# Row norms from statistics, factors in two parts of 16 and 6 tiles, and a mean row summed on VectorE in a two-layer graph kernel

## The chip, the core and the metric

The kernel runs on one core of a Trainium2 chip. A core has five engines with a queue of instructions each: TensorE (PE, with the weight load PEld beside it), VectorE (DVE), ScalarE (ACT), GpSimd (POOL) and SyncE (SP), which issues transfers. Every engine takes its instructions in order, and an instruction waits until what it reads has been written and the buffer that it writes is free. The metric is the time of one execution on the device in microseconds, lower is better.

## The reference

Two layers work on 2,708 rows of 256 numbers and a 2,708 x 2,708 graph. Each is an attention over the graph and then a mixture of experts with two experts for every row. The change lies in layer 1's attention, which works in hyperbolic space:

```
c = float(k)                                   # 1
logx = logmap0(x, c)                           # acosh(x[:,0]) * y / |y|, y = x[:,1:]
Wx = logx[:, 1:] @ W_gcn
tmp = concatenate([0, Wx])
fun7 = proj(expmap0(tmp, c), c)
h_in = logmap0(fun7, c)
h = h_in @ W_att
e = h @ a_att[:F_] + (h @ a_att[F_:]).T
att = softmax(where(adj > 0, e, MASK_FILL), axis=1)
emb = proj(elu(att @ h), c)
out = expmap0(sigmoid(logmap0(emb, c)), c)
```

with x the layer-normed rows. All the maps only scale a row, so `h` of a row is the row through one joined matrix, times a factor that is worked out from three numbers: the row's first element, the norm of its other elements, and the norm of its projection without the second matrix. The softmax's weight then splits: a term that depends on the row read is folded into that row's factor `p_scale`, and the rest drops out. A row with no neighbour gets the mean of all `h`; it comes in through an additional row of the last column with a tiny weight.

## The kernel before

**Tiles.** The rows lie in 22 tiles of 128 (the last two have 74), `tiles`; two neighbours are a pair, 11 in all. `LAST` is 21. The mask of the graph stands in SBUF as `mask_t`, one byte each. Column j of a row tile i is the part of the mask between the tiles j and i.

**Queues.** Instructions of TensorE, VectorE, ScalarE and SyncE keep the order in which the program issues them (L152); those of GpSimd are put in order by the scheduler. Work up to the attention is issued by `Turns`: pieces are generators, each `step()` advances every due piece to its next `yield`, older pieces first. From the attention's third tile on, work is issued by `Clock`: each piece names an engine and an estimated time before it issues, and the planner takes the piece that could start first; `Slots` and `Mark` stand for buffers and events in it. Its estimates set only the order.

**Preparing layer 1.** While layer 0's last experts run, `ahead` (L1461) normalizes the first four pairs and takes the squares of their rows on ScalarE (`square_rows`, L1456) into `norms[:, 0]`. After layer 0 a table of functions is loaded into ScalarE (L1513). `prepare1` adds the two sums of a pair on GpSimd, takes its statistics, and normalizes it on VectorE; `project1` (L1563) turns the pair on TensorE, copies it to `xts` on ScalarE, squares its rows there, projects it (8 matmuls into `u_ps`, of which there are three), squares the projection into `norms[:, 1]` and evicts it to `h_all`. The loop at L1666 starts a pair at each step. In steps 6 to 9 it widens the mask of the row tiles 0 and 1 from bytes to words (`widen`, L1521): the odd columns on GpSimd, the even ones on ScalarE. There are four such half masks.

**Factors.** `factors1(lo, n)` (L1592) turns the three numbers of n tiles into `scale` and `p_scale`: some 35 small VectorE instructions in a chain, with a logarithm and exponents on ScalarE in between. Before, it runs for tiles 0 to 11 within the loop (`FIRST` is 12), started after step 11, and for 12 to 21 after it. `split` (L1634) writes `h * p_scale` of a tile as a rounded half (ScalarE) and its remainder (VectorE), which are the two operands `halves` of the attention.

**Attention.** `sum_up(i, j)` (L1644) adds column j to row tile i with two matmuls of 258 columns. There are three accumulators of the tag `acc` in PSUM. The program issues columns 0 to 11 for the row tiles 0 and 1, then `add_h` (L1653), 44 matmuls that sum `scale * h` of all rows into the mean row, then the second splits, the last column with the mean row in its partitions 64 to 95 (L1691), and the columns 12 to 21. `attention` (L1750) goes on with tile 2 to 21, each with even columns first; `widener` widens the masks, `finish1` (L1763) closes a tile (reciprocal, activation, sum of squares). When the six tiles of a group are closed, `points1` takes them to the router; after the second group (tiles 0 to 11) the first expert blocks of layer 1 are planned, fetched and run.

Of the kernel before, what the change touches and what calls it, by code (L numbers as in the profile page):

```python
# [9 lines left out]
F32 = mybir.dt.float32  # L10
F32R = mybir.dt.float32r
# [11 lines left out]
P = 128  # L23
# [123 lines left out]
def kernel(  # L147
# [260 lines left out]
    def log1p(u):  # L408

        t = ts(u, 1.0, OP.add)  # L410
        k = ts(t.bitcast(I32), 23, OP.logical_shift_right, dtype=I32)
        down = ts(k, -1.0, OP.mult, 254.0, OP.add, dtype=I32)
        scale = ts(down, 23, OP.logical_shift_left, dtype=I32).bitcast(F32)
        m = tt(tt(u, scale, OP.mult), ts(scale, -1.0, OP.add), OP.add)
        z = tt(m, recip(ts(m, 2.0, OP.add)), OP.mult)
        z2 = tt(z, z, OP.mult)
        terms = [2.0 / (2 * n + 1) for n in range(8)]
        q = ts(z2, terms[7], OP.mult)
        for c in reversed(terms[1:7]):
            q = sts(q, c, OP.add, z2, OP.mult)  # L420
        q = sts(q, terms[0], OP.add, z, OP.mult)
        return tt(ts(k, -127.0, OP.add, math.log(2.0), OP.mult), q, OP.add)
# [1033 lines left out]
    def square_rows(xp, pair):  # L1456
        for q, (t, r) in enumerate(pair):
            nc.scalar.activation(row_tile("junk", 4)[:r, 1:], xp[q][:r, 1:], AF.Square,
                                 accum_out=norms[:r, 0, t:t + 1])

    def ahead(b):  # L1461
# [21 lines left out]
        if left == 0:  # L1483
            for k, pair in enumerate(pairs[:AHEAD - 1]):
                square_rows(normed[k], pair)
# [24 lines left out]
    halves = [att.tile([P, T, D + 2], F32R, name=f"half{k}") for k in range(2)]  # L1510
    zeros = filled("zeros", 0.0, T, pool=att)
# [51 lines left out]
    def project1(pair, xp):  # L1563
        ps = ps_tile("tr_ps", "tr").rearrange("p (t c n) -> p t c n", c=DC, n=P)
        for q, (t, r) in enumerate(pair):
            turn_rows(xp[q][:r], r, ps[:, q])
            nc.gpsimd.tensor_copy(c0[:r, t:t + 1], xp[q][:r, 0:1])
        yield 1
        xt = row.tile([P, 2, DC, P], F32, name="xts", bufs=2)
        if pair[1][1] == P:  # L1570
            nc.scalar.copy(xt, ps)
        else:
            for q, (t, r) in enumerate(pair):
                nc.scalar.copy(xt[:, q, :, :r], ps[:, q, :, :r])
        if pairs.index(pair) >= AHEAD - 1:
            square_rows(xp, pair)
        yield 1
        us = []
        for q, (t, r) in enumerate(pair):
            us.append(ps_tile("u_ps", "u"))  # L1580
            project(us[q][:r], xt[:, q], w1x, r)
        yield 1
        for q, (t, r) in enumerate(pair):
            nc.scalar.activation(row_tile("junk", 4)[:r, 1:], us[q][:r, :D - 1], AF.Square,
                                 accum_out=norms[:r, 1, t:t + 1])
            nc.scalar.copy(h_all[:r, t, :], us[q][:r, D - 1:])  # L1586
# [5 lines left out]
    def factors1(lo, n):  # L1592
# [3 lines left out]

# [8 lines left out]
        yield 1  # L1605
        y = newton(v, y)
        u = tt(tt(v[:, :n], y[:, :n], OP.mult), d, OP.add)
        f = tt(log1p(u), y[:, n:2 * n], OP.mult)
        wx = tt(tt(v[:, 2 * n:], y[:, 2 * n:], OP.mult), f, OP.mult)
        part = sts(wx, LEAST, OP.max, recip(ts(wx, MIN_NORM, OP.max)), OP.mult)  # L1610
        tt(part, f, OP.mult, scale[:, lo:hi])
        score = tt(scale[:, lo:hi], h_all[:, lo:hi, D], OP.mult)
        nc.scalar.activation(p_all[:, lo:hi], score, AF.Exp)
        yield 1
# [29 lines left out]
    def sum_up(i, j):  # L1644
# [3 lines left out]
        for half_k in halves:  # L1648
            nc.tensor.matmul(accs[i][:, :D + 2], wide_masks[i, j % 2][:k, j // 2, :],  # L1649
# [3 lines left out]
    def add_h(mean, lo, hi):  # L1653

        for t, r in tiles[lo:hi]:
            nc.tensor.matmul(mean[:96, :D], scale[:r, t:t + 1].to_broadcast([r, 96]),
                             h_all[:r, t, :D], start=t == 0, stop=t == LAST)

    turns = Turns()
    FIRST = 12  # L1660
# [6 lines left out]
    for k in range(17):  # L1667
# [3 lines left out]
        if 6 <= k < 10:  # L1671
            widen(k % 2, k < 8)

        if k == FIRST // 2 - AHEAD + 10:
            turns.start(factors1(0, FIRST))
        if k >= 14:
            lo = 4 * (k - 14)
            split_h(lo, lo + 4)
    split_h(lo + 4, FIRST)
    turns.start(factors1(FIRST, T - FIRST))  # L1680
    turns.finish()
    psum_stage(wide=5, acc=3)
    mean = ps_tile("mean_ps")
# [3 lines left out]
    add_h(mean, 0, T)  # L1687
    split_h(FIRST, FIRST + 4)
    split_h(FIRST + 4, LAST)
    nc.scalar.preload_act_table_set(TANH_TABLE)  # L1690
    split(LAST, slice(64, 96), mean[64:96, :D], TINY / N)  # L1691
    split(LAST, slice(0, TAIL), h_all[:TAIL, LAST, :D], p_scale[:TAIL, LAST:])
    for part in range(2):
        for t in range(FIRST + part, T, 2):
# [55 lines left out]
    def attention():  # L1750
        for i in range(2, T):
            acc_slots[i] = yield from acc.get()
            accs[i] = ps_tile("att_ps", "acc")
            for part in range(2):
                yield wide_at[i, part]
                for j in range(part, T, 2):
# [3 lines left out]
            clock.start(finish1(*tiles[i]), 0)  # L1760
        att_scope.close()
        late_pools()
        clock.set(started)  # L1763

# [255 lines left out]
    for t in range(2):  # L2020
        clock.start(finish1(*tiles[t]), 0)
# [56 lines left out]
```

## Time and profile before

| what | value |
|---|---|
| median of three runs | 1162.97 us (1161.6 to 1166.65) |
| the profiled execution | 1136.56 us, its span 1134.8 us |
| mean granted clock of TensorE | 0.958 |
| layer 0's last expert matmul starts | 657.50 us after the span's start |
| projections of layer 1 | 662.2 to 708.8 us |
| attention of layer 1 on TensorE | 710.4 to 862.5 us |
| first expert block of layer 1 on TensorE | 880.05 us |
| last expert output read by VectorE | about 1094 us |

In the lines of the timeline the columns are the start and the duration in microseconds, the engine, the source line, the operation, what is written and read with its size, how many instructions are merged, and in brackets the idle time of the engine before them and what ended it. The granted clock of a stretch is a share of full speed. The profiled execution is 26.4 us, 2.3%, below the median of the timed runs, so differences are taken within the trace and then laid on the median.

### The profile page before, as it was taken

What the parts mean: (1) busy time and instruction counts of PE and PEld (TensorE: products, weight loads), DVE (VectorE), ACT (ScalarE), POOL (GpSimd) and SP (SyncE); (2) the same over time, 40 slices, a digit from 0 to 9 for tenths busy, and PEclk for the clock granted to TensorE, in tenths of its full rate; (3) what the DMA queues carried; (4) which work ended last, traced back from release to release, by engine and by line L of the source; (5) the groups of instructions that cost most, each with busy time, mean ns of one, the idle gap of its engine ahead of it and who ended that gap; (6) DMA issues with size and microseconds to landing.
All of it is one profiled execution on the core that took longest, in us unless ns stands there. A gap on an engine that the chain in (4) does not pass through costs nothing. (4 is left out here: it accounts for less than half of the span.)

```text
span 1134.8 us, 21254 instructions
## 1 busy us (share of the span) xinstructions
PE 1023.5 (90%) x6665; PEld 909.0 (80%) x6665; DVE 541.9 (48%) x2083; ACT 572.7 (50%) x1599; POOL 367.1 (32%) x417
## 2 busy tenths in 40 slices
PE   5999999998999999999999999998984888999950
PEld 3788888886889999999998853898984787898840
DVE  7778888887420111111111235647777552122368
ACT  4867667664524444444443357536754543444320
POOL 7531112111242222212222350253345166433442
PEclk9999999999989999999999999999897889999985
DMA  9965354431889999999899959400225477787974
GB/s 289 288 242 177 136 175 156 166 95 58 303 251 295 327 326 322 323 306 321 257 311 335 340 160 278 150 1 6 76 84 153 124 215 188 187 213 178 282 194 133
DMA packets 165461, 238.96 MB, mean 211 GB/s; under 512 B 11035, under 2 KB 140374, under 8 KB 162632
## 3 DMA queue, kind: packets, MB, share of 16 engines
q1 hardware_dynamic: 146524, 214.09, 57.9%
q0 software_dynamic: 18816, 23.42, 10.6%
q8 instruction: 56, 0.92, 0.3%
q14 instruction: 65, 0.53, 0.2%
HBM read 205.54 MB, written 54.99 MB: 230 GB/s over the span
## 5 line engine op out<-in xcount | busy, mean ns | idle before, releaser
L911 DVE TENSOR_SCALAR yo<-out_ps,w 128x256 f32<-128x256 f32 x92 | 44.5, 483 | 402.4 <-PE out_ps L905 401.9
L1246 PE MATMUL att_ps<-g_all,z 128*128 128x257 f32 (+3 forms) x968 | 223.6, 383 | 0.0
L905 PE MATMUL out_ps<-room,ht 128*128 128x256 f32 x872 | 201.1, 383 | 0.0
L1246 PEld LDWEIGHTS att_ps<-g_all,z 128*128 128x128 f32 (+3 forms) x968 | 174.9, 186 | 29.6 <-issue 3.1
L887 PEld LDWEIGHTS hid_ps<-xt,room 128*128 128x128 f32 x1504 | 176.4, 193 | 7.3 <-issue 2.5
L887 PE MATMUL hid_ps<-xt,room 128*128 128x128 f32 x1504 | 177.7, 277 | 4.2 <-DMA room<-in_L_ffn_W_dram 3.7
L905 PEld LDWEIGHTS out_ps<-room,ht 128*128 128x128 f32 x872 | 162.7, 192 | 21.3
L1232 ACT ACTIVATE zr<-e_bc,minus_one,g_all 128x256 f32<-128x256 f32 (+3 forms) x242 | 130.4, 591 | 46.4 <-DVE z L1235 45.8
L916 POOL DMA_INDIRECT sums<-yo,xg x43 | 66.8, 1554 | 235.0 <-DVE side L879 173.4
L891 ACT ACTIVATE ht<-hid_ps,w_t 128x128 f32<-128x128 f32 x376 | 128.7, 364 | 28.0 <-PE hid_ps L887 8.8
L681 POOL DMA_INDIRECT rows_d<-xr,place x88 | 92.2, 1048 | 121.0 <-DVE xr L450 76.9
L1649 PE MATMUL att_ps<-half,wide_mask 128*128 128x258 f32 (+1 forms) x968 | 124.5, 290 | 2.5 <-ACT h_all L1586 1.5
L1649 PEld LDWEIGHTS att_ps<-half,wide_mask 128*128 128x128 f32 (+1 forms) x968 | 121.5, 195 | 3.9 <-ACT h_all L1586 2.4
L1235 DVE SCALAR_TENSOR_TENSOR z<-zr,mask_t 128x256 f32<-128x256 f32 (+3 forms) x242 | 96.9, 422 | 29.6 <-ACT zr L1232 18.3
L916 POOL DMA_INDIRECT sums<-yo,xr x45 | 70.6, 1569 | 118.0 <-DMA sums<-yo,xr 30.0
L891 ACT ACTIVATE ht<-hid_ps,w1x 128x128 f32<-128x128 f32 x180 | 62.4, 363 | 88.6 <-PE hid_ps L887 85.0
L881 ACT ACTIVATE w<-xg,side 128x1 f32<-128x1 f32 x43 | 12.7, 294 | 169.2 <-DVE side L879 169.2
L1525 POOL CAST wide_mask<-mask_t 128x1408 fp32r<-128x1408 fp8e4 x31 | 42.5, 1375 | 101.6 <-PE att_ps L1649 67.5
L887 PE MATMUL hid_ps<-lo,wide_mask 128*128 128x128 f32 x480 | 63.4, 287 | 5.6 <-DMA wide_mask<-in_L_ffn_w_dram 4.7
L887 PEld LDWEIGHTS hid_ps<-lo,wide_mask 128*128 128x128 f32 x480 | 60.6, 200 | 9.4 <-issue 6.5
L905 PE MATMUL out_ps<-wide_mask,ht 128*128 128x256 f32 x240 | 59.6, 393 | 0.0
L468 PE MATMUL tr_ps<-ident,xr 128*128 128x128 f32 (+1 forms) x214 | 38.2, 289 | 22.2 <-DMA xr<-rows_d 13.9
(292 smaller groups left out, 1325.0 us busy)
## 6 DMA issues: line engine op xcount, KB each, us to landing
room<-in_L_ffn_W_dram SPq DMA_DIRECT2D x94, 1024.0 KB
wide_mask<-in_L_ffn_w_dram SPq DMA_DIRECT2D x60, 512.0 KB
room<-in_adj_dram SPq DMA_DIRECT2D x20, 1354.0 KB
room<-in_L_ffn_w_dram SPq DMA_DIRECT2D x30, 512.0 KB
rows_d<-nobody SPq DMA_DIRECT2D x1, 7511.0 KB
rows_d<-nobody SPq DMA_DIRECT2D x5, 1295.0 KB
sums<-nobody SPq DMA_DIRECT2D x2, 2944.0 KB
xr<-rows_d SPq DMA_DIRECT2D x45, 129.5 KB
```

The source lines that it names most:

```text
L468: nc.tensor.transpose(ps[:, c, :r], src[:, c * P:(c + 1) * P], ident[:r, :r])
L681: ins = nc.gpsimd.indirect_dma_start(out=self.rows_d[:, :], in_=self.rows[t][:r], in_offset=None, out_offset=bass.IndirectOffsetOnAxis(ap= ...
L887: nc.tensor.matmul(ps[:, :P], w1_b[:, c, f * P:(f + 1) * P], xt[:, c, :], start=(c == 0), stop=(c == DC - 1))
L891: nc.scalar.activation(ht[:, f, :], ps[:, :P], self.func, bias=self.bias[:, f, b:b + 1])
L905: nc.tensor.matmul(ps[:, :D], ht[:, f, :], self.rooms[b % 3][1][:, f, :], start=False, stop=(f == self.FC - 1))
L911: nc.vector.tensor_scalar(yo, ps[:, :D], w, None, op0=OP.mult)
L916: ins = nc.gpsimd.indirect_dma_start(out=self.sums[k][:, :], in_=yo, in_offset=None, out_offset=bass.IndirectOffsetOnAxis(ap=self.rows.pop ...
L1232: nc.scalar.activation(zr[:k, :n], e_bc[:k, lo:lo + n], AF.Relu, bias=minus_one[:k], scale=g_all[:k, j, D + 1:D + 2])
L1235: nc.vector.scalar_tensor_tensor(z[:k, :n], zr[:k, :n], 1.0, mask_t[:k, j // 2, lo:lo + n, j % 2], op0=OP.add, op1=OP.mult)
L1246: nc.tensor.matmul(accs[i][:r, :D + 1], z[:k, q * P:q * P + r], g_all[:k, j, :D + 1], start=(j == 0), stop=(j == LAST))
L1525: nc.gpsimd.tensor_copy(m, src)
L1649: nc.tensor.matmul(accs[i][:, :D + 2], wide_masks[i, j % 2][:k, j // 2, :], half_k[:k, j, :], start=(j == 0 and half_k is halves[0]), stop ...
```

## The change

- The squares of the rows on ScalarE go. `factors1` computes the norm from the layer norm's variance and deviation: 256 times variance times deviation squared, less the first element's square.
- `factors1` and `log1p` yield after almost every step. `FIRST` is 16: the first factors cover tiles 0 to 15 and are issued from step 13 on, twelve steps in each round; the second cover 16 to 21, ten of their steps are put between the splits of tiles 6 to 15, and the others behind them.
- All four half masks of row tiles 0 and 1 are widened on GpSimd.
- `add_h` sums `scale * h` tile by tile on VectorE into `h_sum`; one matmul with ones then gives the mean row.
- That matmul stands behind row tile 2, so row tiles 0 to 2 (`OPEN`) get their last column while tile 3 is summed. Their masks for it are copied to `last_masks`, tile 3 takes an accumulator of the other tag, and `finish1` of the three starts after it. The planner is told that VectorE is busy for its first 6 us.

```diff
     def log1p(u):
         t = ts(u, 1.0, OP.add)
+        yield
         k = ts(t.bitcast(I32), 23, OP.logical_shift_right, dtype=I32)
+        yield
...
-    def square_rows(xp, pair):
-        for q, (t, r) in enumerate(pair):
-            nc.scalar.activation(row_tile("junk", 4)[:r, 1:], xp[q][:r, 1:], AF.Square,
-                                 accum_out=norms[:r, 0, t:t + 1])
-
...
-        if left == 0:
-            for k, pair in enumerate(pairs[:AHEAD - 1]):
-                square_rows(normed[k], pair)
...
+    OPEN = 3
...
-        if pairs.index(pair) >= AHEAD - 1:
-            square_rows(xp, pair)
...
+        var, dev, first = ln_a1.mv[:, lo:hi, 1], ln_a1.rstd[:, lo:hi], c0[:, lo:hi]
+        rest = tt(sts(var, float(D), OP.mult, dev, OP.mult), dev, OP.mult)
+        tt(rest, tt(first, first, OP.mult), OP.subtract, norms[:, 0, lo:hi])
+        yield
...
         nc.scalar.activation(y, v, AF.Ln)
         nc.scalar.activation(y, y, AF.Exp, scale=-0.5)
-        yield 1
-        y = newton(v, y)
-        u = tt(tt(v[:, :n], y[:, :n], OP.mult), d, OP.add)
+        yield
+        h = sts(v, 0.0, OP.add, y, OP.mult)
+        yield
...
         for half_k in halves:
-            nc.tensor.matmul(accs[i][:, :D + 2], wide_masks[i, j % 2][:k, j // 2, :],
+            late = j == LAST and i < OPEN
+            nc.tensor.matmul(accs[i][:, :D + 2],
+                             last_masks[i][:k] if late else wide_masks[i, j % 2][:k, j // 2, :],
                              half_k[:k, j, :], start=(j == 0 and half_k is halves[0]),
                              stop=(j == LAST and half_k is halves[1]))
 
-    def add_h(mean, lo, hi):
-
-        for t, r in tiles[lo:hi]:
-            nc.tensor.matmul(mean[:96, :D], scale[:r, t:t + 1].to_broadcast([r, 96]),
-                             h_all[:r, t, :D], start=t == 0, stop=t == LAST)
+    def add_h(h_sum, t, r):
+        if t == 0:
+            nc.vector.tensor_scalar(h_sum, h_all[:, t, :D], scale[:, t:t + 1], None, op0=OP.mult)
+        else:
+            nc.vector.scalar_tensor_tensor(h_sum[:r], h_all[:r, t, :D], scale[:r, t:t + 1],
+                                           h_sum[:r], op0=OP.mult, op1=OP.add)
 
     turns = Turns()
-    FIRST = 12
+    FIRST, START1 = 16, 13
...
-    for k in range(17):
+    near = factors1(0, FIRST)
+    for k in range(18):
...
         if 6 <= k < 10:
-            widen(k % 2, k < 8)
-
-        if k == FIRST // 2 - AHEAD + 10:
-            turns.start(factors1(0, FIRST))
-        if k >= 14:
-            lo = 4 * (k - 14)
-            split_h(lo, lo + 4)
-    split_h(lo + 4, FIRST)
-    turns.start(factors1(FIRST, T - FIRST))
+            widen(k % 2, k < 8, pool=True)
+        if k >= START1:
+            for _ in range(12):
+                next(near, None)
+    for _ in near:
+        pass
     turns.finish()
     psum_stage(wide=5, acc=3)
-    mean = ps_tile("mean_ps")
+    far = factors1(FIRST, T - FIRST)
+    for t in range(FIRST):
+        split_h(t, t + 1)
+        if t >= 6:
+            next(far)
+    for _ in far:
+        pass
     for j in range(FIRST):
         for i in range(2):
             sum_up(i, j)
-    add_h(mean, 0, T)
-    split_h(FIRST, FIRST + 4)
-    split_h(FIRST + 4, LAST)
+    split_h(FIRST, LAST)
+    h_sum, last_masks = xr_tile()[:, :D], []
+    for i in range(OPEN):
+        if i % 2 == 0:
+            two = xr_tile().bitcast(F32R)
+        last_masks.append(two[:, i % 2 * P:(i % 2 + 1) * P])
+        nc.gpsimd.tensor_copy(last_masks[i], mask_t[:, LAST // 2, i * P:(i + 1) * P, 1])
     nc.scalar.preload_act_table_set(TANH_TABLE)
-    split(LAST, slice(64, 96), mean[64:96, :D], TINY / N)
-    split(LAST, slice(0, TAIL), h_all[:TAIL, LAST, :D], p_scale[:TAIL, LAST:])
+    for t, r in tiles:
+        add_h(h_sum, t, r)
     for part in range(2):
-        for t in range(FIRST + part, T, 2):
+        for t in range(FIRST + part, LAST, 2):
             for i in range(2):
                 sum_up(i, t)
         widen(2, part)
...
     def attention():
+        last_at = Mark()
         for i in range(2, T):
-            acc_slots[i] = yield from acc.get()
-            accs[i] = ps_tile("att_ps", "acc")
+            acc_slots[i] = yield from (bank if i == OPEN else acc).get()
+            accs[i] = ps_tile("att_ps", "wide" if i == OPEN else "acc")
             for part in range(2):
                 yield wide_at[i, part]
-                for j in range(part, T, 2):
+                for j in range(part, LAST if i < OPEN else T, 2):
                     yield "PE", 0.265
                     sum_up(i, j)
                 clock.set(wide_slots[i, part])
-            clock.start(finish1(*tiles[i]), 0)
+                if i == OPEN - 1 and part:
+                    slot = yield from bank.get()
+                    ps = ps_tile("mean_ps")
+                    yield "PE", 0.45
+                    nc.tensor.matmul(ps[:96, :D], ones_f, h_sum, start=True, stop=True)
+                    clock.set(h_sum_slot)
+                    clock.start(split_last(ps, slot, last_at), 0)
+                if i == OPEN and not part:
+                    yield last_at
+                    for k in range(OPEN):
+                        yield "PE", 0.265
+                        sum_up(k, LAST)
+                        clock.start(finish1(*tiles[k]), 0)
+                    for slot in last_mask_slots:
+                        clock.set(slot)
+            if i >= OPEN:
+                clock.start(finish1(*tiles[i]), 0)
...
+    def split_last(ps, slot, mark):
+        yield "ACT", 0.4
+        by = TINY / N
+        nc.scalar.activation(halves[0][64:96, LAST, :D], ps[64:96, :D], AF.Copy, scale=by)
+        yield "DVE", 0.5
+        nc.vector.scalar_tensor_tensor(halves[1][64:96, LAST, :D], ps[64:96, :D], by,
+                                       halves[0][64:96, LAST, :D].bitcast(F32),
+                                       op0=OP.mult, op1=OP.subtract)
+        clock.set(slot)
...
-    for t in range(2):
-        clock.start(finish1(*tiles[t]), 0)
+    clock.free["DVE"] = 6.0
+    h_sum_slot, *last_mask_slots = [xrs.take() for _ in range(1 + (OPEN + 1) // 2)]
     clock.start(widener())
     clock.start(attention(), 2)
```

More of the change, by code (lines that the diff above doesn't have):

```diff
@@ L410, in log1p @@
         t = ts(u, 1.0, OP.add)
+        yield
         k = ts(t.bitcast(I32), 23, OP.logical_shift_right, dtype=I32)
+        yield
         down = ts(k, -1.0, OP.mult, 254.0, OP.add, dtype=I32)
+        yield
         scale = ts(down, 23, OP.logical_shift_left, dtype=I32).bitcast(F32)
-        m = tt(tt(u, scale, OP.mult), ts(scale, -1.0, OP.add), OP.add)
-        z = tt(m, recip(ts(m, 2.0, OP.add)), OP.mult)
+        yield
+        m, less = tt(u, scale, OP.mult), ts(scale, -1.0, OP.add)
+        yield
+        m = tt(m, less, OP.add)
+        yield
+        z = ts(m, 2.0, OP.add)
+        yield
+        z = recip(z)
+        yield
+        z = tt(m, z, OP.mult)
+        yield
         z2 = tt(z, z, OP.mult)
+        yield
         terms = [2.0 / (2 * n + 1) for n in range(8)]
@@ L419, in log1p @@
         for c in reversed(terms[1:7]):
+            yield
             q = sts(q, c, OP.add, z2, OP.mult)
-        q = sts(q, terms[0], OP.add, z, OP.mult)
-        return tt(ts(k, -127.0, OP.add, math.log(2.0), OP.mult), q, OP.add)
+        yield
+        q, k = sts(q, terms[0], OP.add, z, OP.mult), ts(k, -127.0, OP.add, math.log(2.0), OP.mult)
+        yield
+        return tt(k, q, OP.add)
     class Norm:
@@ L1594, in factors1 @@
         hi = lo + n
+        var, dev, first = ln_a1.mv[:, lo:hi, 1], ln_a1.rstd[:, lo:hi], c0[:, lo:hi]
+        rest = tt(sts(var, float(D), OP.mult, dev, OP.mult), dev, OP.mult)
+        tt(rest, tt(first, first, OP.mult), OP.subtract, norms[:, 0, lo:hi])
+        yield
         d = ts(c0[:, lo:hi], -1.0, OP.add, THETA_EPS, OP.max)
@@ L1604, in factors1 @@
         nc.scalar.activation(y, y, AF.Exp, scale=-0.5)
-        yield 1
-        y = newton(v, y)
-        u = tt(tt(v[:, :n], y[:, :n], OP.mult), d, OP.add)
-        f = tt(log1p(u), y[:, n:2 * n], OP.mult)
-        wx = tt(tt(v[:, 2 * n:], y[:, 2 * n:], OP.mult), f, OP.mult)
+        yield
+        h = sts(v, 0.0, OP.add, y, OP.mult)
+        yield
+        h = sts(h, -0.5, OP.mult, y, OP.mult)
+        yield
+        y = sts(h, 1.5, OP.add, y, OP.mult)
+        yield
+        u = tt(v[:, :n], y[:, :n], OP.mult)
+        yield
+        u = tt(u, d, OP.add)
+        log = yield from log1p(u)
+        f = tt(log, y[:, n:2 * n], OP.mult)
+        wx = tt(v[:, 2 * n:], y[:, 2 * n:], OP.mult)
+        yield
+        wx = tt(wx, f, OP.mult)
+        yield
         part = sts(wx, LEAST, OP.max, recip(ts(wx, MIN_NORM, OP.max)), OP.mult)
+        yield
         tt(part, f, OP.mult, scale[:, lo:hi])
+        yield
         score = tt(scale[:, lo:hi], h_all[:, lo:hi, D], OP.mult)
         nc.scalar.activation(p_all[:, lo:hi], score, AF.Exp)
-        yield 1
+        yield
         tt(p_all[:, lo:hi], scale[:, lo:hi], OP.mult, p_scale[:, lo:hi])
@@ L1763, in attention @@
         clock.set(started)
+    def split_last(ps, slot, mark):
[7 more added lines that the diff above has]
+        clock.set(slot)
+        yield "ACT", 0.4
+        lo, by = slice(0, TAIL), p_scale[:TAIL, LAST:]
+        nc.scalar.activation(halves[0][lo, LAST, :D], h_all[lo, LAST, :D], AF.Copy, scale=by)
+        yield "DVE", 0.5
+        nc.vector.scalar_tensor_tensor(halves[1][lo, LAST, :D], h_all[lo, LAST, :D], by,
+                                       halves[0][lo, LAST, :D].bitcast(F32),
+                                       op0=OP.mult, op1=OP.subtract)
+        clock.set(mark, 0.3)
     def finish1(t, r):
```

## The prediction

> **What bounds the kernel now.** The page came first: TensorE is busy for 90% of the span, so anything that leaves its queue looks like a gain.
>
> ```profile
> PE 1023.5 (90%) x6665; PEld 909.0 (80%) x6665; DVE 541.9 (48%) x2083; ACT 572.7 (50%) x1599; POOL 367.1 (32%) x417
> ```
>
> The share is an average, so I cut the stage that the change touches into windows (columns: stretch, its length, busy time and count of PE, PEld, DVE, ACT, POOL, then granted clock, DMA share, GB/s).
>
> ```profile
> 684.00:709.00 25.00, 22.98 (x64) 9.94 (x64) 14.52 (x72) 19.73 (x77) 1.96 (x8) 1.00 1.09 287
> 709.00:732.00 23.00, 21.61 (x143) 18.98 (x144) 16.13 (x71) 13.32 (x34) 2.81 (x2) 1.00 0.56 188
> 732.00:752.00 20.00, 20.00 (x169) 20.00 (x168) 6.70 (x13) 7.99 (x23) 11.04 (x9) 1.00 0.00 1
> 863.00:880.00 17.00, 2.45 (x12) 2.29 (x12) 11.94 (x55) 3.02 (x12) 7.86 (x8) 0.55 0.80 230
> ```
>
> In the projections, the first sums and tiles 2 to 5 TensorE is full. At 863 to 880 it is nearly empty: it waits for the first expert block, which needs tiles 0 to 11 routed. So what counts is when tile 5 and then tile 11 leave attention, not when attention ends. Then the timeline of TensorE:
>
> ```profile
> 706.90 1.94 PE L473 MATMUL u_ps<-w1x,xts 128*74 128x512 f32 x4 [0.91 <-ACT h_all L1586]
> 710.37 6.01 PE L1649 MATMUL att_ps<-half,wide_mask 128*128 128x258 f32 x48 [1.53 <-ACT h_all L1586]
> 716.22 9.91 PE L1656 MATMUL mean_ps<-h_all,scale 128*96 128x256 f32 x44
> 725.78 19.50 PE L1649 MATMUL att_ps<-half,wide_mask 128*128 128x258 f32 x159
> ```
>
> Two sums for columns 0 to 11, 9.91 us of mean row, then attention without a pause. Beside it the timeline of VectorE, from the first factor step on the second tail to the last splits:
>
> ```profile
> 713.96 0.17 DVE L377 TENSOR_SCALAR stat<-c 128x10 f32<-128x10 f32 x1
> ...
> 723.13 0.25 DVE L1590 TENSOR_SCALAR half<-half 32x1 fp32r<-32x1 f32 x2
> 723.41 3.65 DVE L1636 SCALAR_TENSOR_TENSOR half<-h_all,p_scale,half 128x256 fp32r<-128x256 f32 x9
> ```
>
> The second factors run from 713.96 to 723.4 and their splits to 727.06. The mean row on TensorE (716.22 to 726.1) lies exactly over this chain: it is cover, not waste. No matmul of column 12 or later could have started before 723.9.
>
> **What the Trainium skill says.** "SBUF — State Buffer", section "Who interferes with whom": VectorE and GpSimd share a port pair as an exclusive lock; a VectorE instruction with two SBUF inputs contends with a GpSimd instruction that reads SBUF, and the loser blocks wholly. The trace agrees:
>
> ```profile
> 784.13 1.37 POOL L1525 CAST wide_mask<-mask_t 128x1408 fp32r<-128x1408 fp8e4 x1 [3.94 <-PE att_ps L1649]
> 784.21 1.56 DVE L1858 SCALAR_TENSOR_TENSOR h_all<-h_all,common,xr 128x256 f32<-128x256 f32 x1
> ...
> 791.09 1.56 DVE L387 SCALAR_TENSOR_TENSOR stat<-stat,stat 128x6 f32<-128x6 f32 x8
> ...
> 830.29 4.69 DVE L387 SCALAR_TENSOR_TENSOR stat<-stat,stat 128x6 f32<-128x6 f32 x8
> 831.89 2.67 POOL L1525 CAST wide_mask<-mask_t 128x1408 fp32r<-128x1408 fp8e4 x2
> ```
>
> The L1858 instruction has a median of 0.47 us and took 1.56 under the cast, +1.08; another at 825.34 took 1.85, +1.38; eight small steps took 4.69 us instead of 1.56 under two casts; the casts keep their 1.37. "TensorE: Matmul & The Clock Gate", section "What's actually happening": after an idle window of about 3.4 us the clock falls to half, and sustained work of that length restores it. The trace agrees: after 4.73 us of idle time the next stretch ran at 0.50:
>
> ```profile
> 790.00:795.00 5.00, 0.27 (x4) 0.80 0.01 2
> 795.00:798.00 3.00, 3.00 (x14) 0.50 0.58 197
> ```
>
> **The change, part by part** (times on the trace's axis).
>
> *Row norms from statistics.* 22 squares leave ScalarE, about 0.41 us each (8 took 3.3 us from 658.43), 9 us. Two mask casts of 1.36 us (685.78 and 688.76) go to GpSimd, idle from 680 but for 0.5 us copies. On the path this is worth only what TensorE waited for: 0.6 at the stage's start (the table load stood behind 8 squares), 0.65 at 690.8, 0.91 at 706.9. Projections end at 708.84 - 2.2 = 706.6. Four small VectorE steps come in for each factor call, 0.7 us.
>
> *Factors for 16 tiles.* They now stand behind step 13, so the logarithm follows the eviction of tile 17 and the copies of the last pair on ScalarE. Tile 17's projection ended at 700.5 (696.93 and 3.60); now at 699.3, two of the three waits being ahead of it. Eviction 0.9, copies 0.5, logarithm and exponent 0.5: 701.1, where before VectorE went on at 699.2. From there 8.0 us as before (699.20 to 707.17): the factors end at 709.1, and the first sum starts at about 709.2 instead of 710.37, with TensorE idle for 2.6 us. The yields hide nothing here, since VectorE has no other work between.
>
> *Splits and ten steps of the second factors.* 16 splits at 0.41, first statistics 0.65, ten steps at about 0.1 to 0.3 between them, and one wait of VectorE for a logarithm that stands in ScalarE's queue between splits (about 0.9): split 15 ends at 719.0. TensorE needs 64 matmuls x 0.1225 (19.50 over 159) = 7.8 us, so it is paced by VectorE and ends at 719.5.
>
> *The rest of the second factors.* Before, from the tenth step (716.9) to 723.4: 6.5 us. Nothing lies between now and TensorE has no mean row to do: it idles from 719.5 to 725.6. Splits 16 to 20 end at 727.6, as late as before. Columns 16 to 20 take 2.45 us, up to twice that at half clock: done at about 730.5, where before the same point with the last column was 731.2. The 9.9 us taken off TensorE have bought under 1 us.
>
> *The sum on VectorE.* It is queued behind split 20: one 0.41, then 21 instructions in a chain through `h_sum`. A dependent 128x256 instruction with a pointer scalar follows after 0.51 (L1858 at 780.97, its reader at 781.48): 11.1 us, so 738.7 uncovered. Lower bound 22 x 0.41 = 9.0, if the chain cost nothing. In that stretch GpSimd casts five half masks (second half of tile 2, both of tile 3, both of tile 4, each as TensorE frees a buffer), and each instruction here has two SBUF inputs. Bounds: 0 if GpSimd gives way, 5 x 1.38 = 6.9 if it always wins. I take 5 x 1.2 = 6.0, since every cast in the dense stretches after 780 kept its time: h_sum at 744.7.
>
> *The added wait.* The mean matmul stands on TensorE behind tile 2 and ahead of tile 3. Tile 2 takes 42 x 0.1225 = 5.15 us, to 735.8. TensorE then waits 9 us for h_sum with tile 3, the late columns and all of attention behind it. Then 0.5 for the matmul, 5.4 for tile 3 and 0.74 for three late columns; `split_last` (about 2 us on ScalarE and VectorE) hides under tile 3's first half of 2.7. Half clock after the wait: 3.4 to 5 us at half rate, +1.7 to +2.4. Tile 3 ends at 744.7 + 0.5 + 6.1 + 2 = 753.3; before 741.5. That is +11.8.
>
> *Onwards.* `finish1` of tiles 0 to 2 comes late, but tile 5 ends last of its group either way, 10.6 us after tile 3. Group 1's chain and the 220 us of experts follow in series, and the tail from 1100 runs off VectorE; I see no slack to absorb it and take off 0.3 for rounding. Sum: 1136.56 + 11.5 = 1148.1 for the profiled execution. The median of the runs shown is 1162.97, 2.3% above that execution; with the same addition it is 1174.5.
>
> **The rivals.** *The sum is late by its own length alone* (casts do not hold it): h_sum 738.7, wait 3, tile 3 at 745.3, +4 to +5 with some half clock: 1167.5. For: the added buffers could shift the casts. Against: L1858. *The sum is hidden:* it needs h_sum by 735.8, which asks for 8 us from 727.6, below the bound of 9.0: then +0 to +1, 1163.5. *Faster:* the mean row's 44 matmuls were on the path, and TensorE starts attention sooner. This decides from the point where splits 16 to 20 end before about 722 and h_sum ends within tile 2; then at most 9.9 - 0.5 - 0.9 us come off: 1154.5. For: TensorE at 90%. Against: the second factors, whose 9.4 us are serial and need VectorE from 712 on. *Worse:* the hand-planned order behind puts TensorE's transposes in front of late work, as at 790 (4.73 us idle), a second time: +18, 1181.
>
> **How the numbers follow.** Forecast 0.57, late by its own length 0.20, hidden 0.08, faster 0.08, worse 0.07. About 0.5% (5.8 us) is what a measurement here can tell from no change. Slower: 0.57 + 0.07 + half of the second case = 0.74; same: the rest of it and hidden, 0.18; faster 0.08. The forecast's own bounds (casts 0 to 6.9, half clock 1.7 to 3.4, start of the first sum ±1) give +7 to +15; reaching down to the second case and up to the worse one, 1164 to 1182.
>
> **What would show it.** Right: a TensorE idle stretch near 719 to 725 ended by a split, and a longer one before the mean matmul ended by VectorE's `h_sum`; instructions of `h_sum` of over 1 us beside GpSimd casts; half clock after it. Wrong: `h_sum` spaced at 0.41 to 0.45 with no wait behind tile 2; splits 16 to 20 before 722; or a first expert block as early as 880 in spite of a late tile 3.

## The result, and the profile after

The changed kernel takes 1174.07 us (median of four runs, 1173.52 to 1177.81) beside 1164.4 us of the kernel before (median of four, 1161.6 to 1166.65): a ratio of 1.0093, with a 95% interval of 1.0064 to 1.0122. It is slower, by 9.7 us. A later measurement, on a chip where the kernel before takes 1137.25 us, gave 1.0088 (1.0060 to 1.0116).

The profiled execution took 1173.97 us, its span 1172.3. The first row of the page shows that TensorE has lost share, from 90% to 88%, though the change took 42 of the mean row's 44 matmuls off it:

```profile
PE 1026.0 (88%) x6623; PEld 912.0 (78%) x6623; DVE 556.3 (47%) x2113; ACT 561.7 (48%) x1553; POOL 371.2 (32%) x422
```

In this trace the projections (first matmul into `u_ps`) start at 668.65, before at 663.84: the axis is shifted by 4.8 us, for a reason that lies ahead of the projections. What follows is therefore told from the start of the projections. The windows of the stage, cut near the ends of its steps (same columns as in the prediction):

```profile
689.00:711.60 22.60, 22.49 (x64) 10.11 (x64) 12.54 (x61) 12.03 (x48) 2.60 (x11) 1.00 1.09 283
711.60:731.00 19.40, 11.92 (x68) 11.45 (x69) 16.53 (x85) 10.54 (x29) 0.00 (x0) 0.73 0.85 266
731.00:748.20 17.20, 8.61 (x61) 8.39 (x60) 16.36 (x25) 2.31 (x2) 7.22 (x5) 0.80 0.00 0
748.20:757.00 8.80, 8.80 (x60) 8.57 (x61) 3.09 (x10) 3.80 (x10) 2.00 (x2) 0.83 0.01 3
```

Where TensorE was full before, it is now busy for 11.92 of 19.40 us and for 8.61 of 17.20; VectorE is the busiest engine there, 16.53 and 16.36. The granted clock is 0.73 to 0.83 in the stretches with the pauses and behind them. The timeline of TensorE shows the same as waits:

```profile
704.51 7.08 PE L489 MATMUL u_ps<-w1x,xts 128*128 128x512 f32 x16
714.44 10.63 PE L1673 MATMUL att_ps<-half,wide_mask 128*128 128x258 f32 x64 [2.85 <-ACT half L1658]
729.10 0.58 PE L1673 MATMUL att_ps<-half,wide_mask 128*128 128x258 f32 x1 [4.03 <-ACT half L1658]
730.29 9.29 PE L1673 MATMUL att_ps<-half,wide_mask 128*128 128x258 f32 x61 [0.61 <-DVE half L1659]
748.17 1.17 PE L1799 MATMUL mean_ps<-xr,ones_f 128*96 128x256 f32 x2 [8.59 <-DVE xr L1682]
```

Four waits: 2.85 us for the first factors, 4.03 and 0.61 for the second ones, 8.59 for the sum on VectorE. In the trace of before these places held 1.53 us and the mean row. The last wait is made by VectorE and GpSimd together. Their timelines follow: first VectorE with the last of the second factors' splits and the sum, then GpSimd's casts:

```profile
729.75 2.06 DVE L1659 SCALAR_TENSOR_TENSOR half<-h_all,p_scale,half 128x256 fp32r<-128x256 f32 x5
731.74 0.35 DVE L1680 TENSOR_SCALAR xr<-h_all,scale 128x256 f32<-128x256 f32 x1
732.12 15.99 DVE L1682 SCALAR_TENSOR_TENSOR xr<-h_all,scale,xr 128x256 f32<-128x256 f32 x21
```

```profile
733.10 5.86 POOL L1534 CAST wide_mask<-mask_t 128x1408 fp32r<-128x1408 fp8e4 x4 [36.43 <-PE att_ps L1673]
739.72 1.36 POOL L1534 CAST wide_mask<-mask_t 128x1408 fp32r<-128x1408 fp8e4 x1 [0.76 <-PE att_ps L1673]
```

The view of the source line gives the smallest, median and largest time of one instruction of the sum in nanoseconds:

```profile
L1682 DVE SCALAR_TENSOR_TENSOR xr<-h_all,scale,xr x21: 479/485/1572, 732.1 to 747.6; 128x256 f32<-128x256 f32 x19, 74x256 f32<-74x256 f32 x2
```

Most instructions take 485 ns; five, each beside one of the five casts, take 1,460 to 1,572. Row tile 5, the last of its group, is closed (its reciprocal starts) 98.20 us after the start of the projections, before 88.35. The timelines of VectorE, before and then after:

```profile
752.19 0.17 DVE L1772 RECIPROCAL inv<-att_ps 128x2 f32<-128x2 f32 x1 [2.75 <-PE att_ps L1649]
```

```profile
766.85 0.17 DVE L1841 RECIPROCAL inv<-att_ps 128x2 f32<-128x2 f32 x1 [2.75 <-PE att_ps L1673]
```

That is +9.85 us, about the whole difference of the timed runs.

The difference of the two profiled executions is 37.4 us, not 9.7. Most of the rest lies in three places: layer 0, and two pauses of TensorE that the first trace of before does not have; the second profiles of both kernels, further down, deal with them.

### The profile page after: what moved, and what is told of

Same layout as the page of the kernel before. It is cut to its first block, busy times and chain, and to the rows that moved or that the text cites. A ratio compares the mean times of both kernels' runs of the same rounds, so it can differ in the third digit from the quotient of the medians.

```text
span 1172.3 us, 21138 instructions
## 1 busy us (share of the span) xinstructions
PE 1026.0 (88%) x6623; PEld 912.0 (78%) x6623; DVE 556.3 (47%) x2113; ACT 561.7 (48%) x1553; POOL 371.2 (32%) x422
## 5 line engine op out<-in xcount | busy, mean ns | idle before, releaser
L1673 PE MATMUL att_ps<-half,wide_mask 128*128 128x258 f32 (+1 forms) x962 | 130.8, 298 | 10.3 <-ACT half L1658 6.9
L1673 PEld LDWEIGHTS att_ps<-half,wide_mask 128*128 128x128 f32 (+1 forms) x962 | 127.2, 204 | 12.1 <-issue 6.6
L1534 POOL CAST wide_mask<-mask_t 128x1408 fp32r<-128x1408 fp8e4 x33 | 45.8, 1395 | 114.0 <-PE att_ps L1673 113.9
```

Source lines behind the costliest of these rows:

```text
L1534: nc.gpsimd.tensor_copy(m, src)
L1673: nc.tensor.matmul(accs[i][:, :D + 2], last_masks[i][:k] if late else wide_masks[i, j % 2][:k, j // 2, :], half_k[:k, j, :], start=(j == 0 ...
```

## The experiments

Two numbers stand for each: the ratio to the kernel before, timed on the same chip, and the time from the start of the projections to the closing of row tile 5 in its profile (before: 88.35 and, in a second profile, 88.36). The experiments ran on three chips; so only the ratios and the times from the start of the projections are compared across them. The row of the changed kernel is its second measurement.

| kernel | ratio (95% interval) | tile 5 closed | against before |
|---|---|---|---|
| changed | 1.0088 (1.0060 to 1.0116) | 98.58 us | +10.2 |
| casts on ScalarE | 1.0038 (1.0019 to 1.0057) | 93.31 | +5.0 |
| sum of one tile | 0.9987 (0.9966 to 1.0007) | 89.02 | +0.7 |
| mean row back on TensorE | 1.0000 (0.9982 to 1.0019) | 89.11 | +0.8 |
| norms alone | 0.9982 (0.9965 to 0.9999), again 0.9996 (0.9976 to 1.0016) | 87.20, 87.20 | -1.1 |
| four open tiles | 1.0091 (1.0063 to 1.0119) | 95.85 | +7.5 |
| four open tiles, casts on ScalarE | 1.0002 (0.9981 to 1.0022) | 88.24 | -0.1 |
| shared mean row, casts on ScalarE | 1.0002 (0.9984 to 1.0021) | 88.98 | +0.6 |
| norms alone, later transposes | 0.9976 (0.9960 to 0.9993) | 87.14 | -1.2 |

The first four split the change's cost.

**The casts that hold VectorE.** The changed kernel, with the half masks of row tiles 2 to 4 cast on ScalarE instead of GpSimd:

```diff
-        if part or pool:
+        if (part or pool) and not 2 <= i < 5:
...
-        pool = part or i < POOL_WIDENS
+        pool = i >= 5 and (part or i < POOL_WIDENS)
```

> The changed kernel with the half masks of row tiles 2 to 4 cast on ScalarE, so that GpSimd casts nothing while VectorE sums the rows. Lock theory (the casts hold the sum up): the 21 chained steps go from 15.99 us to about 10.7, h_sum is done some 5 us earlier, TensorE's wait in front of the mean matmul falls from 8.6 to about 3.5 us, and the time falls by 5 to 6 us, to about 1168.5. Rival (the sum is late by its own length, the casts fill pauses): the 21 steps stay at 15 to 16 us and the time at about 1174.

Measured 1.0038. The timeline of VectorE, then the view of the source line, then the wait in TensorE's timeline:

```profile
728.66 10.90 DVE L1682 SCALAR_TENSOR_TENSOR xr<-h_all,scale,xr 128x256 f32<-128x256 f32 x21
```

```profile
L1682 DVE SCALAR_TENSOR_TENSOR xr<-h_all,scale,xr x21: 479/485/487, 728.7 to 739.1; 128x256 f32<-128x256 f32 x19, 74x256 f32<-74x256 f32 x2
```

```profile
739.61 0.95 PE L1799 MATMUL mean_ps<-xr,ones_f 128*96 128x256 f32 x2 [2.45 <-DVE xr L1682]
```

The median stays at 485 ns and the largest falls to 487: all the long instructions were those beside a cast. The chain of 21 takes 10.90 us instead of 15.99, so five casts held it for 5.09 us, 1.02 each, and the wait falls from 8.59 to 2.45. About half of the change's cost goes with it: 1.0088 becomes 1.0038, and tile 5 is 5.0 us late instead of 10.2.

**A sum of one tile.** In the changed kernel 21 of the 22 tiles are left out of the mean row; all else, the late columns too, stays:

```diff
-    for t, r in tiles:
-        add_h(h_sum, t, r)
+    add_h(h_sum, *tiles[0])
```

> The changed kernel with only row tile 0 in the sum; the other 21 tiles are left out of the mean row. Theory (the sum on VectorE is what delays attention): no wait in front of the mean matmul, no half clock after it, row tile 3 ends about 10 us earlier than in the changed kernel, time about 1164, the time of the kernel before. Rival (the pauses after the span's 880th microsecond, or the new order of the planner, make the loss): at most 3 us come back, time about 1171.

Measured 0.9987. The mean matmul follows tile 2 without a wait, though the casts are on GpSimd and the three late columns are still late:

```profile
735.68 0.59 PE L1798 MATMUL mean_ps<-xr,ones_f 128*96 128x256 f32 x2
```

The late columns, `split_last` and the moved `finish1` thus cost nothing that the timed runs show (tile 5 is closed 0.7 us later than before); the rest of the cost is the sum's own length. Without the casts it is worth 1.0038 - 0.9987, 0.5% or 5.9 us of 1158.27 us.

**The mean row back on TensorE.** The changed kernel, but with the 44 matmuls behind columns 0 to 15 as cover and no open tiles:

```diff
-    OPEN = 3
...
+    add_h(mean, 0, T)
     split_h(FIRST, LAST)
...
-    for t, r in tiles:
-        add_h(h_sum, t, r)
...
```

> The changed kernel with the mean row back on TensorE as 44 matmuls behind columns 0 to 15 and all row tiles closed in order; norms from statistics and factors for 16 and 6 tiles stay. Cover theory (the mean row lay over the second factors): it takes the 4 us for which TensorE now waits on the splits of tile 16 on, and of its 9.9 us about 6 remain on the path; first sum as in the changed kernel, row tile 3 ends 0 to 2 us later than in the kernel before, time about 1165. Rival (taking it off TensorE is worth its 9.9 us): about 1174 plus something, no better than the changed kernel.

Measured 1.0000, as the cover theory had it. In TensorE's timeline the mean row starts as column 15 ends and the attention follows it without a wait:

```profile
722.30 9.68 PE L1679 MATMUL mean_ps<-h_all,scale 128*96 128x256 f32 x44
731.63 48.56 PE L1671 MATMUL att_ps<-half,wide_mask 128*128 128x258 f32 x399
```

Columns from 16 on run 64.51 us after the start of the projections (731.63 - 667.12); in the changed kernel, with no mean row in front of them, they run, but for one matmul 1.2 us ahead, from 61.64 (730.29 - 668.65). Taking 9.7 us of work off TensorE brought this point forward by 2.9 us; the expectation had about 6.

**The norms alone.** The kernel before, with the row norms from statistics and all first casts on GpSimd, but 12 tiles in the first factors and the mean row on TensorE:

```diff
-            nc.scalar.activation(row_tile("junk", 4)[:r, 1:], xp[q][:r, 1:], AF.Square,
-                                 accum_out=norms[:r, 0, t:t + 1])
...
+        tt(rest, tt(first, first, OP.mult), OP.subtract, norms[:, 0, lo:hi])
...
-            widen(k % 2, k < 8)
+            widen(k % 2, k < 8, pool=True)
```

> The kernel before with the first part of the change alone: row norms from statistics, no squares on ScalarE, all four first half masks cast on GpSimd. Factors for 12 and 10 tiles, mean row on TensorE. Theory: the projections end 2.2 us earlier and, as the logarithm isn't pushed back, the first sum starts 2 to 3 us earlier; TensorE has no pause up to tile 11, so 2 to 3 us come off the kernel before: about 1162. Rival (the four added steps and the factors set the start): the first sum starts within 0.5 us of before and the time is 1164.

Measured 0.9982. A second measurement of the same kernel:

> The kernel before with only the row norms from statistics and all first casts on GpSimd, a second time and perhaps on another chip. Theory (the stage before the first sum is 1.8 us shorter and nothing else changes): 0.997 to 0.9995. Rival (the first ratio of 0.9982 was chance): 0.9995 or more.

Measured 0.9996, on the rival's side of the line that I had drawn. Both profiles agree with each other: from the start of the projections to the first sum 44.77 and 44.78 us, before 46.53 in both of its profiles. Not all of these 1.75 us last. In TensorE's timeline the mean row now has a wait, behind 24 of its 44 matmuls:

```profile
709.80 6.02 PE L1642 MATMUL att_ps<-half,wide_mask 128*128 128x258 f32 x48 [1.53 <-ACT h_all L1576]
715.66 5.35 PE L1649 MATMUL mean_ps<-h_all,scale 128*96 128x256 f32 x24
721.60 4.54 PE L1649 MATMUL mean_ps<-h_all,scale 128*96 128x256 f32 x20 [0.59 <-issue]
```

Tile 5 is closed 1.15 us earlier than before, 0.10%, which is less than the timed runs can tell: both intervals are compatible with it and the second with nothing.

The next four ask whether the wait explains the cost that is left; the first two are the two kernels themselves.

**The kernel before and the changed kernel again.**

> The kernel before, unchanged, for a second profile. Theory: the first profile of it (1136.56 us, 26 us under its own timed runs) is an unusual execution, and the pause of TensorE of about 11 us right behind the attention of layer 1 (ended by VectorE's hot_f, with ScalarE and SyncE's transfer late at the same moment) and one of 7 to 8 us later (ended by ScalarE's w1x), which every later profile has, belong to every usual execution of the kernel before too: this profile shows both, and 1150 to 1166 us. Rival: the change makes these pauses: this profile shows neither, and about 1137 us, and the change would then cost far more than 1%.

> The changed kernel, unchanged, beside the other experiments. Theory: 1.008 to 1.010 of the kernel before, as first measured, which is the 9.9 us by which row tile 5 is closed later. Rival (the first ratio came from a few runs and is partly chance): under 1.006.

The kernel before took 1133.98 us in its one profiled execution; the changed one has a median of 1147.62, and the ratio is 1.0088, first 1.0093. Both ideas on the pauses fall: the second profile of before has neither pause, and the changed kernel on this chip has none either. The same matmuls behind the attention in TensorE's timeline, first of the changed kernel's first profile, then of its second one, then of the second of before:

```profile
892.54 1.87 PE L874 MATMUL bias_ps<-hot_f,w1x 16*128 16x8 f32 x8 [12.48 <-DVE hot_f L866]
```

```profile
878.20 1.87 PE L874 MATMUL bias_ps<-hot_f,w1x 16*128 16x8 f32 x8 [2.01 <-DVE hot_f L866]
```

```profile
862.75 1.87 PE L858 MATMUL bias_ps<-hot_f,w1x 16*128 16x8 f32 x8 [1.98 <-DVE hot_f L850]
```

One kernel shows 12.48 us in one execution and 2.01 in another. The pause is a matter of the execution, not of the change. Of the 37.4 us between the first two profiles 5.0 lie in layer 0 (its last expert matmul starts at 657.50 and 662.52), 10.5 are this pause (12.48 - 1.98), of which the next wait gives 2.1 back (12.30 and 10.15), and 6.6 a later one in front of a transpose (8.22 and 1.59). That is 20 us; 9.7 to 11 are the change's, and some 7 us of the experts' stage I have not followed. On this chip, without the pauses, the kernel before has a median of 1137.25 us, on the two others 1158.27 and 1157.8. The two profiles from this chip differ by 13.7 us in span (1146.0 and 1132.3), 4.3 of it ahead of the projections; from there to the end by 9.4.

**Four open tiles.** The mean matmul one row tile later, with tile 3 open too; the casts stay on GpSimd:

```diff
-    OPEN = 3
+    OPEN = 4
...
-            acc_slots[i] = yield from (bank if i == OPEN else acc).get()
+            acc_slots[i] = yield from (bank if 3 <= i <= OPEN else acc).get()
```

> The changed kernel with the mean matmul one row tile later: four tiles are open, it stands behind tile 3 and the late columns behind the first half of tile 4. The casts stay on GpSimd. Theory (TensorE waits for VectorE's sum, and everything behind it moves with the sum): TensorE has another 5.2 us of work ahead of the wait; one more cast may fall into the sum (+1). The wait of 8.6 us shrinks to 3.4 to 4.7, row tile 5 is closed about 5 us later than before instead of 9.9, and the ratio is 1.003 to 1.006. Rival (the cost lies in the late closing of the first tiles and the planner's order behind them, not in the wait): another tile is closed late, and the ratio is 1.009 or more.

Measured 1.0091: my theory's number was missed, the rival's came in. The timelines of TensorE, then of VectorE and then of GpSimd say why:

```profile
723.85 14.37 PE L1673 MATMUL att_ps<-half,wide_mask 128*128 128x258 f32 x103 [0.61 <-DVE half L1659]
743.81 1.17 PE L1799 MATMUL mean_ps<-xr,ones_f 128*96 128x256 f32 x2 [5.59 <-DVE xr L1682]
```

```profile
725.67 18.08 DVE L1682 SCALAR_TENSOR_TENSOR xr<-h_all,scale,xr 128x256 f32<-128x256 f32 x21
...
761.07 1.37 DVE L1848 SCALAR_TENSOR_TENSOR lo<-xn,lo 128x256 f32<-128x256 f32 x1 [0.32 <-ACT lo L1846]
763.53 1.31 DVE L1893 TENSOR_SCALAR stat<-emb_sq 128x6 f32<-128x6 f32 x1 [0.58 <-ACT xn L1853]
```

```profile
726.65 5.86 POOL L1534 CAST wide_mask<-mask_t 128x1408 fp32r<-128x1408 fp8e4 x4 [36.20 <-PE att_ps L1673]
733.31 1.37 POOL L1534 CAST wide_mask<-mask_t 128x1408 fp32r<-128x1408 fp8e4 x1 [0.80 <-PE att_ps L1673]
735.95 1.37 POOL L1534 CAST wide_mask<-mask_t 128x1408 fp32r<-128x1408 fp8e4 x1 [1.27 <-PE att_ps L1673]
738.36 1.49 POOL L1534 CAST wide_mask<-mask_t 128x1408 fp32r<-128x1408 fp8e4 x1 [1.04 <-PE att_ps L1673]
```

TensorE got its 5.2 us of work, but each half tile that it finishes frees a buffer and starts another cast: seven instead of five fell into the sum, which grew from 16.0 to 18.08 us. So the wait is 5.59 us and not 3.4 to 4.7. The 2.7 us that are left at tile 5 (95.85 instead of 98.58) are lost at once: the group's first common step starts 101.33 us after the start of the projections (763.53 - 662.20), in the changed kernel 101.72 (766.35 - 664.63), and tile 11 is closed after 135.8 and 135.7 us. `finish1` of six tiles now comes in a heap ahead of that step. That this heap is what holds the step is read from the timeline and was not tried by itself; it is the part of the rival that holds.

**Four open tiles and no casts on GpSimd.** Both edits together:

> The same with four open tiles, and the half masks of row tiles 2 to 4 cast on ScalarE, so that nothing holds VectorE's sum. Theory: the sum ends about 5 us after tile 2 at the latest and tile 3 gives 5.2 us: no wait is left, or under 0.5 us, the clock stays at full speed behind it, row tile 5 is closed at most 2 us later than before, and the ratio is 0.998 to 1.002. Rival (a sum on VectorE and late columns cost something by themselves): 1.003 or more, as with three open tiles.

Measured 1.0002, the theory's number. The same two views:

```profile
736.48 0.59 PE L1799 MATMUL mean_ps<-xr,ones_f 128*96 128x256 f32 x2
```

```profile
723.90 10.89 DVE L1682 SCALAR_TENSOR_TENSOR xr<-h_all,scale,xr 128x256 f32<-128x256 f32 x21
```

No wait in front of the mean matmul, the sum at its own 10.89 us, tile 5 closed as in the kernel before, and with it all of the change's cost gone, to within 0.2%. Four tiles are open and closed late here too, so that by itself costs nothing that shows. It needed both edits: the casts away alone left 0.38%, the later place alone left everything.

The last two ask whether a version beats both kernels.

**A shared mean row.** Three open tiles, the casts of row tiles 2 to 4 on ScalarE, tiles 0 to 9 of the mean row on TensorE behind column 15, tiles 10 to 21 on VectorE:

```diff
+    ON_PE = 10
...
+    for t, r in tiles[:ON_PE]:
+        nc.tensor.matmul(mean[:96, :D], scale[:r, t:t + 1].to_broadcast([r, 96]),
+                         h_all[:r, t, :D], start=t == 0, stop=False)
     split_h(FIRST, LAST)
...
-    for t, r in tiles:
+    for t, r in tiles[ON_PE:]:
         add_h(h_sum, t, r)
```

> The changed kernel with three open tiles, the half masks of row tiles 2 to 4 cast on ScalarE, and the mean row shared: tiles 0 to 9 on TensorE (20 matmuls, 4.5 us) behind columns 0 to 15, where TensorE waits for the second factors, tiles 10 to 21 on VectorE, both added by the last matmul behind tile 2. Theory (the wait of 4 to 5 us behind column 15 can take TensorE work for nothing, and a sum of 12 tiles ends within tile 2): no wait of over 1 us between the first sum and the transposes of group 0, row tile 5 is closed 1 us earlier to 1 us later than before against the start of the projections, 0.997 to 1.000. Rival (with all waits filled the second factors still set the time, and what is gained there is lost to TensorE's additional work): 1.000 to 1.002.

Measured 1.0002. In TensorE's timeline no wait is over 1 us from the first sum to the transposes of group 0:

```profile
720.75 4.49 PE L1720 MATMUL mean_ps<-h_all,scale 128*96 128x256 f32 x20
726.01 0.39 PE L1673 MATMUL att_ps<-half,wide_mask 128*128 128x258 f32 x1 [0.78 <-ACT half L1658]
727.21 9.73 PE L1673 MATMUL att_ps<-half,wide_mask 128*128 128x258 f32 x61 [0.81 <-DVE half L1659]
736.77 0.59 PE L1804 MATMUL mean_ps<-xr,ones_f 128*96 128x256 f32 x2
```

The waits are as the theory had them; the ratio lies on the rival's side, though its interval holds both. Columns from 16 on begin at 61.67 us, as in the changed kernel (61.64), with 4.49 us more work on TensorE: that much work is free there, and leaving it out gains nothing. The second factors set this point.

**Later transposes.** The norms alone, with the planner's estimate of a small VectorE step raised:

```diff
-        return "DVE", 0.19 * n
+        return "DVE", 0.27 * n
```

> The same, with the planner's estimate of a small VectorE step raised from 0.19 to 0.27 us, so that it puts TensorE's transposes of group 0 behind more of the attention's matmuls. Theory (the wait of 4.74 us of TensorE in front of these transposes is on the path, as the attention behind it delays tile 11 and the second group): the wait goes, the first expert block starts up to 4.7 us earlier, 0.993 to 0.997. Rival (later transposes put the router's steps of both groups later, and the order of the experts behind suffers): 1.000 or more.

Measured 0.9976, between what the theory and the rival expect. In its profile the wait of 4.74 us in front of group 0's transposes is down to 1.15, but new ones follow in TensorE's timeline:

```profile
834.68 15.74 PE L1642 MATMUL att_ps<-half,wide_mask 128*128 128x258 f32 x110 [4.70 <-POOL wide_mask L1517]
...
863.91 0.34 PE L623 MATMUL rank_ps<-hot,tri 128*128 128x192 bf16 x1 [4.20 <-DVE hot L609]
870.62 0.18 PE L826 MATMUL number_ps<-fresh_bf,tri 58*58 58x32 bf16 x1 [5.18 <-DVE fresh_bf L822]
```

and the first expert block starts 228.7 us after the start of the projections, with the norms alone 225.1 and 223.5 in its two profiles, although those two hold the pause of 12.40 and 11.42 us that is told at the end, and this one doesn't. That the wait was on the path is not shown, and the small gain in the timed runs is not explained by this profile. Its interval overlaps with that of the norms alone; it is the fastest kernel of the study against before, by 0.24% (0.07 to 0.40%), and which part of that is the later order stays open.

## Why the prediction was right

The forecast was 1174.5 us, late by the sum and the casts that hold it; measured 1174.07. The likeliest case is the one that came. By its steps, on before's axis (5.0 us are taken off the times of after, since layer 0's last expert matmul starts at 662.52 there and at 657.50 before):

- *Norms.* Projections end at 706.6 as predicted (711.59 - 5.0), though of the 0.6 us at the stage's start only 0.2 came and the rest within the stage. By the experiment with the norms alone this is worth 1.75 us at the first sum and 1.15 at tile 5.
- *First factors.* VectorE goes on at 701.1 (706.07 - 5.0), the first sum starts at 709.4; predicted 701.1 and 709.2. The wait of 2.85 us stands where 2.6 was predicted.
- *Columns 0 to 15* end at 720.1, predicted 719.5. The prediction had VectorE set their pace; here split 15 was done at 718.2 instead of 719.0, and TensorE was still at the columns, at a clock of 0.72 over their 10.63 us. The half clock was reckoned with behind the two later waits only. In the second profile they took 9.56 us, and the wait behind them was 5.10; it ended at the same point, 60.44 us after the start of the projections instead of 60.45, so nothing hung on this.
- *Second factors.* The wait was predicted at 6.1 us and measured at 4.03 and 0.61: VectorE was done with splits 16 to 20 at 726.8 instead of 727.6. Tile 2 started at 729.4, in before at 730.8, and the last column's four matmuls, 0.5 us, were still to come: under 1 us was bought, as predicted. That TensorE has next to nothing to gain here was the core of the argument, and the shared mean row and the mean row back on TensorE show how far it goes: with 4.5 us more work the attention goes on as early (61.67 beside 61.64), with 9.7 us more 2.9 us later (64.51). So the mean row is cover for the larger part of its length, not for all of it.
- *The sum.* Uncovered it was put at 11.1 us; with the casts on ScalarE it took 11.3 (728.28 to 739.56). So the spacing of a dependent instruction, read from another line, carried over.
- *The casts.* Predicted five casts of 1.2 us, 6.0 us; measured five, 5.09 us, 1.02 each. The bounds were 0 and 6.9. This term was 0.9 us too large; the smallest of the cases that the prediction showed, +1.08 us for the instruction at 784.21, would have priced it almost rightly. The statement of the Trainium skill on which it rests ("SBUF — State Buffer", section "Who interferes with whom"), that a VectorE instruction with two SBUF inputs and a GpSimd instruction that reads SBUF contend for one port pair, agrees with this trace: five instructions of VectorE went from 485 to as much as 1,572 ns, and the casts took 1.36 to 1.56 us. Each of the five started after its cast had started (the first at 733.16, its cast at 733.10).
- *The added wait.* Its start was summed up 0.15 us too late (730.5 and 5.15 make 735.65, not 735.8), which changes nothing. Predicted 9 us, measured 8.59, and 2.45 without the casts. Behind it the clock was 0.70 for 5.0 us and 1.00 from then on:

```profile
748.20:753.20 5.00, 5.00 (x29) 4.77 (x30) 0.95 (x3) 0.89 (x2) 0.19 (x1) 0.70 0.02 5
753.20:758.00 4.80, 4.80 (x43) 4.80 (x42) 2.25 (x8) 3.87 (x12) 2.54 (x2) 1.00 0.00 0
```

  A clock of 0.70 over 5.0 us costs 1.5 us, where 2 were taken.
- *Onwards.* Tile 5 was put 11.8 us late and is 9.85 and 10.2 late. "I see no slack to absorb it" holds roughly: on the one chip that has profiles of both kernels, 10.2 us at tile 5 are 11.5 at the first expert block (228.1 us instead of 216.6) and 9.4 at the end of the span, all measured from the start of the projections.

The mechanism was right, and three of its terms were a little too large: the casts' hold by 0.9 us, the end of the splits by 0.8 and the half clock by 0.5; the sum's own length was 0.2 too small. That makes 2.0 us of the 2.2 by which tile 5 is less late on before's axis (9.64 us) than predicted (11.8). In the timed runs +9.7 us were measured where +11.5 were forecast. That the total nevertheless met 1174.07 within half a microsecond is luck: the median of the runs before rose by 1.4 us, from 1162.97 to 1164.4, with one more run.

The rivals: the sum late by its own length alone was the experiment with the casts on ScalarE, 1.0038 or about +4.4 us, as that rival's +4 to +5 had it. The hidden sum needs more than the change gives; with four open tiles and the casts away it is there, at 1.0002. The faster case fails at its own point of decision, splits 16 to 20 ending before about 722: they end at 726.8. A second delay of the transposes did not come: the wait in front of them is 4.75 and 4.73 us in the two profiles of the changed kernel, 4.73 and 4.74 before.

## What to carry to other kernels

Before work is taken off the engine that is busy for 90%, look at what else runs beside it: work that covers a serial chain elsewhere can be free, as 4.49 us of the mean row were here, and moving it onto the engine of that chain puts it on the path. A sum moved to VectorE has to be priced with what GpSimd does at the same time, and that may be work which the fast engine itself triggers by freeing buffers; more cover then brings more of it. When two profiles differ by far more than the timed runs, take a second profile of the kernel before, and measure each stage from its own start, before anything is put down to the change.

## What the runs showed that I had not expected

The pause of TensorE behind the attention is the largest surprise: 11.4 to 12.5 us in the first profile of the changed kernel and in six of the seven profiles from two of the chips, about 2 us in all four from another chip, the same kernel among them. It goes along with medians of the kernel before that are 20 to 21 us apart (1158.27 and 1157.8 beside 1137.25). ScalarE and VectorE stop with TensorE there (11.53 and 10.32 us in the profile of the norms alone), and the trace names no instruction of this core that releases them. The timeline of ScalarE in that profile, where `remote` stands for such a release:

```profile
876.70 0.21 ACT L842 CAST where<-where_ps 1x8 int32<-1x8 f32 x2 [11.53 <-remote]
```

From the 600th us on, waits of ScalarE or VectorE of over 3 us that end so stand in the first profile of the changed kernel and in all seven from the two slower chips, in the norms alone with later transposes at another place (10.86 us on VectorE at 941.29); none stands in the four from the faster chip. The first profile of before has none either and is 26 us under its timed runs. What makes the pause stays open.

Layer 0, in which the change touches next to nothing, ended at different times too: the projections started at 660.37 and 663.84 us in two profiles of the one kernel before, and at 664.63 and 668.65 in two of the changed one. With four open tiles, whose layer 0 is that of the changed kernel, they started at 662.20 and 660.45. So this shift differs between kernels that do the same up to there, and it is not put down to the change; what makes it stays open.
